# A four-layer graph network on one core: smaller reloads, a ring of four for the second step's projections, and one block of casts moved from layer 3 into layer 2's end

## The chip, the cores and the metric

The kernel runs on one core of a Trainium2 chip. The metric is the device time of the whole kernel in microseconds, the median of several runs. A profiled execution gives the span from the first to the last instruction and the trace that the views below are read from. The engines are named as in the profile: PE is TensorE (PEld its weight loads), DVE is VectorE, ACT is ScalarE, POOL is GpSimd, SP is SyncE, which here only issues DMAs.

## The reference

`x` has 4096 rows of 256 features, `adj` is a 4096 × 4096 matrix of zeros and ones. Four layers follow one another, each as `x = layernorm(x + layer(x))`:

```python
# layer 0: attention of 8 heads over the neighbours, softmax of leaky_relu(parent + child)
# layer 1: (diagonal + adj) @ (x @ weight) + bias
# layer 2: two steps
R = S + I;  R = R / R.sum(-1)              # S is adj
for n in range(2):
    A = top_p_attention(Xa, W1, W2, W3)    # softmax of q k^T, kept up to a mass of 0.9, renormalised
    Xf = R @ Xf
    Xa = A @ Xa
    Z = Z + Xf @ U1[n].T + Xa @ U2[n].T
x_out = layernorm_affine(X + Z)
# layer 3
agg = adj @ x / max(deg, 1)
out = relu(concat([x, agg]) @ W + b)
```

## The kernel before

The 4096 rows are 32 blocks of 128 (`NB` = 32). The change lies in layer 2 and at the start of layer 3.

**What is kept where.** `XD` holds, for each block of 128 source rows, two sets of 256 values as the moving operand of the matmuls. `X` holds the current attention features. `es[0..2]` are three tiles of 4096 numbers per partition, one row block of attention scores each, used in turn by row block modulo three. `kT` holds the keys of the step, transposed. `adj_piece` is a ring of three tiles of 256 KB; each takes four 128 × 128 blocks of the adjacency (f32) from DRAM. `work` is the pool of small tiles: `xb` (two buffers), `part` and `dif` (one each), `q` (two).

**One step of layer 2.** The step starts with projections: `project(step, b)` (L1441 to L1481) multiplies two row blocks with the step's weights. In step 1 it also reads back the running sum of these two blocks from DRAM into `xb` (SP, L1476), copies one half of the result into `X` (ACT) and the other into `part` or `dif` (ACT, L1479), adds it to `xb` on POOL (L1480) and writes the sum back with a DMA that POOL issues (L1481). There are sixteen such pairs. Then `keys` fills `kT`, and the main loop goes over row blocks `b`, each in eight slots `s`. In a row, PE computes the scores of row `b+2` (`scores`, L979, with ACT's exponentials L981 into `es[(b+2)%3]`), DVE finds the nucleus of row `b+1`, and PE transposes (`turn`, L1336) and multiplies (`gather`, L1345, eight matmuls) the kept attention of row `b`. Beside it, `diffusion` multiplies adjacency pieces with `XD` for row block `b+2` (step 0) or `b+3` (step 1): `piece` (L1531) issues the DMA on SP, `times` (L1540) the four matmuls. A `pieces` tuple says how many of these stand before the gather of each slot; a piece is loaded two ahead, as the ring has three.

**The order of the work.** Inside `manual_schedule` the order on each engine is the order of the program text. SP's queue is served in order: pieces, reloads, loads of `q` and `xb`, all stand one behind the other there.

**A step's end.** The rows of the last `diffusion` are done before the last attention rows, and `XD` must then be refilled with the results of this step (the next step's or layer 3's operand). `reload(rows_of, from, to)` (L1193 to L1197) brings those blocks from DRAM (`xfd` in step 0, `xtd` in step 1) with one DMA on SP of 256 KB per block. `freed` is a table of the slots (row counted from the end of the diffusion, slot) at which a group of four blocks is fetched. With the new blocks, `early` multiplies the first rows of the next step (step 0: rows 0 to 2) or of layer 3 (step 1: rows 0 to 4) beside the last attention rows: the list `todo` gives their order. The last blocks come by a reload after the loop (`NB - 4` on): in step 0 after `mend`, in step 1 after the last row's pieces.

**Layer 2's end and layer 3.** After the last row's `mend`, step 1 has a stretch of its own (L1764 to L1822): byte loads of the adjacency for layer 3 (`load_bytes`, `nas`), eight gathers of the last row with turns, the closing of rows 29, 30 and 31 (`closing`, `ahead3`, `weighted` L1438), the casts of layer 3's block 5 into `kT` (`cast3` L1842 on ACT), the remaining pieces of `todo`, the product of block 5 in four parts (`product(i)`, L1791, eight matmuls each from `a[i]`), and the last source block's matmuls (L1822) once row 31 is closed. Layer 3 then goes over the row blocks from 6 on: `ready(b)` casts a block's bytes into four `adj_piece` tiles (DVE L1840 and ACT L1842 in turn), `products(b)` makes 32 matmuls (L1873), `close(b)` makes the output rows. Blocks 6 and 7 are made ready ahead of the loop.

Of the kernel before, what the change touches and what calls it, by code (L numbers as in the profile page):

```python
# [9 lines left out]
F32 = mybir.dt.float32  # L10
I32 = mybir.dt.int32
F32R = mybir.dt.float32r
# [43 lines left out]
class Net:  # L56
# [745 lines left out]
    def layer2(self):  # L802
# [3 lines left out]
        with ExitStack() as ctx:  # L806
# [386 lines left out]
            def reload(src, a, b):  # L1193

                for k in range(a, b, 4):
                    to = min(k + 4, b)
                    nc.sync.dma_start(XD[:, k:to].bitcast(F32), src[k:to].rearrange("b p s d -> p b s d"))  # L1197
# [244 lines left out]
            def bank():  # L1442
                return psum.tile([P, 512], F32, name="ps_tp")

            def project(step, b):


                two = slice(b, b + 2)
                rows = lambda t: t.rearrange("b p d -> p b d")
                pl = psum.tile([P, 2, 512], F32, name="ps_logit", bufs=2)  # L1450
                if step == 0 and b < 16:
                    pt = bank()
                    for q in range(2):
                        for c in range(2):
                            nc.tensor.transpose(pt[:, (2 * q + c) * P:(2 * q + c + 1) * P],
                                                X[:, b + q, c * P:(c + 1) * P], self.ident)
                    xT = work.tile([P, 512], F32, name="aT", bufs=2)
                    nc.scalar.copy(xT, pt)
                    xT = xT.rearrange("p (q c m) -> p q c m", q=2, c=2)
                else:  # L1460
                    xT = held(step, b, 2)
                for q in range(2):
                    for c in range(2):
                        nc.tensor.matmul(pl[:, q, :], xT[:, q, c, :], wt[:, c].rearrange("p k m -> p (k m)"),
                                         start=(c == 0), stop=(c == 1))
                xb = work.tile([P, 2, D], F32, name="xb", bufs=2)
                if step == 0:
                    nc.scalar.copy(XD[:, two, 0, :], pl[:, :, :D])
                    nc.scalar.copy(xb, pl[:, :, D:])
                    nc.vector.tensor_sub(XD[:, two, 1, :], pl[:, :, :D], XD[:, two, 0, :].bitcast(F32))  # L1470
                    nc.scalar.dma_start(rows(pd[two]), xb)
                    xs = work.tile([P, 2, D], F32, name="part", bufs=1)
                    nc.gpsimd.tensor_add(xs, X[:, two, :], affine.unsqueeze(1).to_broadcast([P, 2, D]))
                    nc.gpsimd.dma_start(rows(xd[two, :, 1, :]), xs)
                else:
                    nc.sync.dma_start(xb, rows(xd[two, :, 0, :]))  # L1476
                    nc.scalar.copy(X[:, two, :], pl[:, :, :D])
                    xs = work.tile([P, 2, D], F32, name=("part", "dif")[b // 2 % 2], bufs=1)
                    nc.scalar.copy(xs, pl[:, :, D:])  # L1479
                    nc.gpsimd.tensor_add(xb, xb, xs)  # L1480
                    nc.gpsimd.dma_start(rows(xd[two, :, 0, :]), xb)  # L1481
# [23 lines left out]
            def ahead3(b, h, pz, last=False, queue=nc.scalar):  # L1505

                part = XD[:, b] if last else work.tile([P, 2, D], F32, name="part", bufs=1).bitcast(F32R)
                nc.scalar.copy(part[:, 0], pz[:, D:])
                nc.scalar.copy(h[:, 0], pz[:, :D])
                nc.vector.tensor_sub(part[:, 1], pz[:, D:], part[:, 0].bitcast(F32))  # L1510
                yield
                if not last:
                    queue.dma_start(xtd[at(b)].rearrange("o p s d -> (o p) s d"), part.bitcast(F32))
                queue.dma_start(xo[at(b), :, 1].rearrange("o p d -> (o p) d"), h[:, 0])
# [49 lines left out]
            for step in range(2):  # L1564
# [40 lines left out]
                if step == 0:  # L1605
# [3 lines left out]
                dd = 2 + step  # L1609
                rows_of = (xfd, xtd)[step]  # L1610
                banks, made = {}, []
                freed = ((-1, 4), (-1, 5), (-1, 6), (-1, 7), (0, 0), (0, 2), (0, 4)) if step == 0 else \
                    ((0, 4), (-1, 5), (-1, 6), (-1, 7), (0, 0), (0, 2), (1, 1))
                freed = {at: g for g, at in enumerate(freed)}
                if step == 0:
                    todo = [(k, g) for g in range(7) for k in range(3)]
                else:
# [5 lines left out]
                with tc.manual_schedule(engines=five):  # L1623
                    for b in range(NB - 1):
# [14 lines left out]
                        for s in range(8):  # L1639
# [28 lines left out]
                            for _ in range(pieces[s]):  # L1668
                                next(beside)
                            if (b + dd - NB, s) in freed:  # L1670
                                g = freed[b + dd - NB, s]
                                reload(rows_of, 4 * g, 4 * g + 4)
                            gather(pa, aTs.pop(0), s)
                            if s == 3 and step == 1 and b - 2 in done:
                                put = ahead3(b - 2, done.pop(b - 2), pz, queue=nc.gpsimd)
# [87 lines left out]
                with tc.manual_schedule(engines=five):  # L1763
                    nas = [t[:, i * 2048:(i + 1) * 2048].bitcast(U8).rearrange("p (k i) -> p k i", k=8)  # L1764
                           for t in (es[2], es[0]) for i in range(2)]
                    self.load_bytes(nas, 0, 0)
                    xb = bases(b)
                    h = done.pop(b - 2)
                    xT = turned(h[:, 0], bank())
                    pa = ps1.tile([P, 512], F32, name="ps_a")  # L1770
                    aTs = [turn(es[b % 3], 0)]
                    for g in range(8):
                        if g < 7:
                            aTs.append(turn(es[b % 3], g + 1))
                        if g in (0, 6):
                            put = ahead3(b - 2 + g // 6, h, weighted(xT, bank()))
                        gather(pa, aTs.pop(0), g)
                        if g in (0, 3):
                            next(close)
                        if g in (1, 7):  # L1780
                            whole(put)
                        if g == 5:
                            h = whole(close)
                            xT = turned(h[:, 0], bank())
                    close = closing(b, pa, r, xb)
                    ps = ps1.tile([P, 512], F32, name="ps_a")
                    a = [kT[:, i * 1024:(i + 1) * 1024].rearrange("p (k i) -> p k i", k=8) for i in range(4)]

                    def product(i):
                        for jc in range(8 * i, 8 * i + 8 - (i == 3)):  # L1790
                            nc.tensor.matmul(ps, a[i][:, jc % 8, :], XD[:, jc].rearrange("p s d -> p (s d)"),  # L1791
                                             start=(jc == 0), stop=False)

                    next(close)
                    next(close)
                    self.cast3(nas, 5, a, nc.scalar)
                    for _ in range(4):
                        next(beside)
                    next(close)
                    whole(beside)  # L1800
                    reload(xtd, NB - 4, NB - 1)
                    lasts = []
                    for k in range(2):
                        two = work.tile([P, 2, P], F32R, name="q", bufs=2)
                        nc.sync.dma_start(two.bitcast(F32), self.adjs[2 * k:2 * k + 2, :, NB - 1, :].rearrange("b p i -> p b i"))
                        lasts += [two[:, 0], two[:, 1]]
                    rows = [X[:, 8 * i:8 * i + 8, :].rearrange("p b d -> p (b d)").bitcast(U8)
                            .rearrange("p (k i) -> p k i", k=8) for i in range(4)]
                    product(0)
                    for k in range(5):  # L1810
                        t = piece(1, k, 7)
                        times(banks[k], t, 7, ks=range(3))
                    lasts.append(t[:, 3])
                    h = whole(close)
                    product(1)
                    xT = turned(h[:, 0], bank())
                    product(2)
                    pz = weighted(xT, bank())
                    product(3)
                    whole(ahead3(b, h, pz, True))  # L1820
                    for t, to in zip(lasts + [a[3][:, 7]], [banks[k] for k in range(5)] + [ps]):
                        nc.tensor.matmul(to, t, XD[:, b].rearrange("p s d -> p (s d)"), start=False, stop=True)  # L1822
                    self.load_bytes(rows, 1, 0)
                self.ahead3 = nas, rows
                self.early3 = [banks[k] for k in range(5)] + [ps]

    def load_bytes(self, nas, it, g):
# [17 lines left out]
    def layer3(self):  # L1845
        nc, tc, NB, D = self.nc, self.tc, self.NB, self.D
        G = 8
        with self.ctx3 as ctx:
# [6 lines left out]
            out = self.rows(self.out)  # L1855
            psum, ps1 = self.psum2, self.ps2
            nas = self.ahead3
            pieces = {}

            def ready(b):  # L1860
                it = b * P // self.IT
# [26 lines left out]
                self.layernorm(work, y, h)  # L1888
                nc.scalar.dma_start(out[:, b, :], y[:, 0])

            ready(6)
            ready(7)
            rest = [2, 5, 0, 1, 3, 4]
            for b in range(6, NB):
# [61 lines left out]
```

## Time and profile before

| what | value |
| --- | --- |
| median of three runs | 4033.21 us (4031.47 to 4039.32) |
| profiled execution, its own time | 4036.06 us |
| its span | 4034.4 us |
| mean granted PE clock | 0.987 |
| PE busy | 3912.9 us, 97% |
| DVE busy | 2994.1 us, 74% |
| ACT busy | 2757.1 us, 68% |
| POOL busy | 1088.5 us, 27% |
| step 0's end | about 2590 to 2720 us of the span |
| projections and keys of step 1 | about 2720 to 2835 us |
| loop of step 1 | about 2835 to 3790 us, 30.46 us a row |
| layer 2's end, then layer 3 | from about 3790 us; layer 3 from 3828 us |

The page of the profile gives busy times for the whole span. The views by window give waits ("engine, what ran, line, then what it waited for and its line: us in total, times, longest us"), and the timeline gives the start, the length, the engine, the line, the operation, output and inputs, shapes, the number of instructions taken together and, in brackets, the idle time before them and what ended it. In two rows of step 1, from 2900.00 to 2960.92 us, PE is busy all the time, DVE for 58.58, ACT for 53.71 and POOL for 34.40 us.

### The profile page before, as it was taken

Reading aid. Unit: us, or ns where it says so; the run is one execution under the profiler, and the core shown is the slowest. Engines: PE = TensorE matmul, PEld = TensorE weight load, DVE = VectorE, ACT = ScalarE, POOL = GpSimd, SP = SyncE. Lnnn points to the kernel's source line nnn. Section 1 sums busy time; section 2 is a strip of 40 time slices with the busy share of each in tenths; the row PEclk is TensorE's granted clock in tenths of the full one; section 3 lists DMA queues with packets and bytes.
Section 4 is the critical chain, followed back from the end, with each engine's and each line's share of the span. In section 5 each row is a group of like instructions: output and inputs, shape, how many; then the busy total and the mean of one; then the engine's idle time right before and its main releaser. Section 6 shows DMA issues by size and latency. Waiting matters only on the chain. (4 is left out here: it accounts for less than half of the span.)

```text
span 4034.4 us, 68767 instructions
## 1 busy us (share of the span) xinstructions
PE 3912.9 (97%) x25081; PEld 3383.5 (84%) x25081; DVE 2994.1 (74%) x6643; ACT 2757.1 (68%) x5127; POOL 1088.5 (27%) x1333
## 2 busy tenths in 40 slices
PE   8999999999999999899999999989999999999899
PEld 7899999999999788578888888865888888888687
DVE  7642328999999444567878788737899999999364
ACT  5543339999999322468888888825988888888132
POOL 0111110111333122301111111114555555555211
PEclk9999999999999999999999999999999999999999
DMA  4665547334222597432333232453333333335541
GB/s 136 224 214 175 178 147 228 93 101 131 69 76 64 192 369 311 131 115 95 98 97 101 95 104 92 146 190 100 103 116 103 106 119 99 107 120 188 185 152 47
DMA packets 320570, 556.42 MB, mean 138 GB/s; under 512 B 71558, under 2 KB 146198, under 8 KB 316118
## 3 DMA queue, kind: packets, MB, share of 16 engines
q1 hardware_dynamic: 239920, 395.13, 30.2%
q0 software_dynamic: 28336, 86.42, 6.5%
q10 hardware_dynamic: 51958, 70.29, 5.1%
q8 instruction: 203, 3.33, 0.3%
q14 instruction: 153, 1.25, 0.1%
HBM read 385.78 MB, written 165.94 MB: 137 GB/s over the span
## 5 line engine op out<-in xcount | busy, mean ns | idle before, releaser
L1345 PE MATMUL ps_a<-X,aT 128*128 128x256 f32 x4096 | 973.4, 380 | 1.3 <-ACT h L1486 1.1
L1345 PEld LDWEIGHTS ps_a<-X,aT 128*128 128x128 f32 x4096 | 776.5, 190 | 128.2 <-issue 3.5
L320 PE MATMUL acc<-gm,gt 128*128 128x198 bf16 x8192 | 706.2, 249 | 22.0 <-DMA gm<-gmd 6.8
L320 PEld LDWEIGHTS <-gt 128*128 128x128 fp8e4 x8192 | 702.8, 98 | 25.4 <-issue 9.8
L267 ACT ACTIVATE sg<-lpb,nlc 128x1024 fp8e4<-128x1024 f32 x636 | 667.2, 1135 | 61.5 <-DVE gt L269 39.8
L180 PE MATMUL ps_r<-XD,adj_piece 128*128 128x512 f32 x1888 | 528.4, 414 | 0.3 <-DMA adj_piece<-adjs 0.3
L538 PE MATMUL pz<-src,ar 128*128 128x264 f32 x4096 | 510.2, 287 | 15.2 <-DVE ar L528 12.7
L538 PEld LDWEIGHTS pz<-src,ar 128*128 128x128 f32 x4096 | 507.1, 190 | 18.1 <-DVE ar L528 11.6
L1072 ACT ACTIVATE ja<-e,nc 128x2048 uint8<-128x2048 f32 x240 | 480.9, 2004 | 2.0
L1338 ACT COPY aT<-ps_tp 128x512 f32<-128x512 f32 x512 | 296.4, 579 | 222.5 <-PE ps_tp L1336 220.5
L180 PEld LDWEIGHTS ps_r<-XD,adj_piece 128*128 128x128 f32 x1888 | 332.9, 189 | 69.3 <-issue 12.9
L531 ACT ACTIVATE nb<-a 128x512 uint8<-128x512 f32 x256 | 156.4, 630 | 287.7 <-DMA a<-in_adjt_dram 274.7
L1137 DVE MAX8 cand<-v 128x8 f32<-128x256 f32 x1024 | 347.3, 412 | 4.4
L1187 DVE SCALAR_TENSOR_TENSOR e<-e,edge 128x512 f32<-128x512 f32 x512 | 347.3, 750 | 2.2
L1336 PE MATMUL ps_tp<-ident,e 128*128 128x128 f32 x2048 | 307.9, 273 | 0.0
L1133 DVE SCALAR_TENSOR_TENSOR v<-e,hi 128x2048 f32<-128x2048 f32 x128 | 300.7, 2350 | 2.4
L1336 PEld LDWEIGHTS ps_tp<-ident,e 128*128 128x128 f32 x2048 | 257.1, 142 | 51.4 <-issue 0.7
L261 DVE TENSOR_SCALAR sg<-lpb,nlc 128x1024 fp8e4<-128x1024 f32 x384 | 285.4, 779 | 5.9 <-DVEq L358 3.9
L979 PE MATMUL ps_logit<-kT,q 128*128 128x512 f32 x1024 | 276.8, 412 | 12.4 <-DVE kT L937 8.0
L981 ACT ACTIVATE e<-ps_logit 128x1024 f32<-128x1024 f32 x256 | 260.2, 1027 | 30.3 <-PE ps_logit L979 30.3
L528 DVE CAST ar<-a 128x1024 fp32r<-128x1024 f32 x128 | 88.6, 693 | 231.0 <-PE pz L538 229.9
L790 PE MATMUL ps_adj<-XD,adj_piece 128*128 128x512 f32 x1024 | 244.9, 399 | 0.0
(397 smaller groups left out, 5543.7 us busy)
## 6 DMA issues: line engine op xcount, KB each, us to landing
adj_piece<-adjs SPq DMA_DIRECT2D x552, 256.0 KB, 2.7
a<-in_adjt_dram SPq DMA_DIRECT2D x256, 256.0 KB, 3.0
adjs<-adj_piece SPq DMA_DIRECT2D x96, 512.0 KB, 4.8
na<-nad SPq DMA_DIRECT2D x64, 512.0 KB, 3.7
nad<-nb POOLq DMA_DIRECT2D x128, 128.0 KB, 3.3
lpb<-lpd POOLq DMA_DIRECT2D x32, 512.0 KB, 4.1
na<-nad ACTq DMA_DIRECT2D x16, 1024.0 KB, 6.9
gmd<-gb ACTq DMA_DIRECT2D x64, 198.0 KB, 3.3
```

The costliest lines, as they stand in the source:

```text
L180: nc.tensor.matmul(ps, a[:, k, :], rhs(jc).rearrange("p s d -> p (s d)"), start=(jc == 0), stop=(jc == self.NB - 1))
L261: nc.vector.tensor_scalar(sg[:, k, :], lpb, nlc[:, 4 * g + k, h:h + 1], 2.0 ** -5, op0=ALU.is_ge, op1=ALU.mult, saturate=False)
L267: nc.scalar.activation(sg[:, k, :], lpb, AF.Sign, scale=-1.0, bias=nlc[:, 4 * g + k, h:h + 1], saturate=False)
L320: nc.tensor.matmul(acc[:, q, :6 * C1], gt[:, k, q * P:(q + 1) * P], gm0[:, k, :] if head0 else gm[:, jc, hh, :], start=(jc == 0 and q % 2 ...
L538: nc.tensor.matmul(pz[q][:, t, :W], ar[:, q, k, :], src[:, jc, t, s], start=(jc == 0 and s == 0), stop=(jc == NB - 1 and s == 1))
L1072: nc.scalar.activation(ja, e[:, s * HALF:(s + 1) * HALF], f, bias=nc1, accum_out=fs[:, i + s:i + s + 1])
L1133: nc.vector.scalar_tensor_tensor(v, ec, hi, ec, op0=ALU.is_lt, op1=ALU.mult, accum_out=sb[:, s:s + 1])
L1137: nc.vector.max(cand[:, 8 * j:8 * j + 8], v[:, k * 256:(k + 1) * 256])
L1187: nc.vector.scalar_tensor_tensor(ec, ec, edge[:, j:j + 1], ec, op0=ALU.is_ge, op1=ALU.mult)
L1336: nc.tensor.transpose(pt[:, k * P:(k + 1) * P], e[:, jc * P:(jc + 1) * P], self.ident)
L1338: nc.scalar.copy(aT, pt)
L1345: nc.tensor.matmul(pa[:, :D], aT[:, k * P:(k + 1) * P], X[:, jc, :], start=(jc == 0), stop=(jc == NB - 1))
```

## The change

There are three parts, all in layer 2 and its passage to layer 3.

1. In `project`, step 1, the pairs 2 to 12 take `xb` and the copied half from slots of `es[2]`, four deep each, in place of the work tiles `xb` (two buffers) and `part`/`dif` (one each). Pairs 0, 1 and 13 to 15 keep those.
2. `freed` gives a range of blocks for each slot. In step 0 the first 28 blocks come in ten reloads of one to four blocks where there were seven of four; in step 1 in twelve reloads of two or three blocks where there were seven of four.
3. In layer 2's end three pieces of `early` are multiplied between gathers (slots 3, 5, 7); blocks 28, 29 and 30 of `XD` are reloaded one by one (after gathers 2 and 4, and ahead of the last pieces) where one reload of three stood; the two loads of `q` tiles stand at gather 3; and the four casts of layer 3's block 6 are made there by ACT, into the `kT` tiles that `product` has read. Layer 3 starts with these (`pieces = {6: self.sixth}`) and makes only block 7 ready ahead of its loop.

```diff
@@ project
-                xb = work.tile([P, 2, D], F32, name="xb", bufs=2)
+                nth = (b - 16) % NB // 2
+                ring = [es[2][:, i + nth % 4 * 512:i + nth % 4 * 512 + 512].rearrange("p (q d) -> p q d", d=D)
+                        for i in (0, 2048)] if step and 2 <= nth <= 12 else ()
+                xb = ring[0] if ring else work.tile([P, 2, D], F32, name="xb", bufs=2)
...
-                    xs = work.tile([P, 2, D], F32, name=("part", "dif")[b // 2 % 2], bufs=1)
+                    xs = ring[1] if ring else work.tile([P, 2, D], F32, name=("part", "dif")[b // 2 % 2], bufs=1)
@@ main loop
-                freed = ((-1, 4), (-1, 5), (-1, 6), (-1, 7), (0, 0), (0, 2), (0, 4)) if step == 0 else \
-                    ((0, 4), (-1, 5), (-1, 6), (-1, 7), (0, 0), (0, 2), (1, 1))
-                freed = {at: g for g, at in enumerate(freed)}
+                if step == 0:
+                    freed = {(-1, 4): (0, 4), (-1, 5): (4, 7), (-1, 6): (7, 10), (-1, 7): (10, 14), (0, 0): (14, 18),
+                             (0, 1): (18, 21), (0, 2): (21, 23), (0, 3): (23, 25), (0, 4): (25, 27), (0, 5): (27, 28)}
+                else:
+                    freed = {(-1, 5): (4, 7), (-1, 6): (7, 10), (-1, 7): (10, 13), (0, 0): (13, 16), (0, 1): (16, 18),
+                             (0, 2): (18, 20), (0, 3): (20, 22), (0, 4): (22, 24), (0, 5): (0, 2), (0, 6): (2, 4),
+                             (1, 1): (24, 26), (1, 2): (26, 28)}
...
-                                g = freed[b + dd - NB, s]
-                                reload(rows_of, 4 * g, 4 * g + 4)
+                                reload(rows_of, *freed[b + dd - NB, s])
@@ layer 2's end
+                        if g in (3, 5, 7):
+                            next(beside)
                         gather(pa, aTs.pop(0), g)
+                        if g in (2, 4):
+                            k = NB - 5 + g // 2
+                            reload(xtd, k, k + 1)
+                        if g == 3:
+                            lasts = []
+                            for k in range(2):
+                                two = work.tile([P, 2, P], F32R, name="q", bufs=2)
+                                nc.sync.dma_start(two.bitcast(F32),
+                                                  self.adjs[2 * k:2 * k + 2, :, NB - 1, :].rearrange("b p i -> p b i"))
+                                lasts += [two[:, 0], two[:, 1]]
...
-                    for _ in range(4):
+                    for _ in range(3):
                         next(beside)
                     next(close)
+                    reload(xtd, NB - 2, NB - 1)
                     whole(beside)
-                    reload(xtd, NB - 4, NB - 1)
-                    lasts = []
-                    for k in range(2):
-                        two = work.tile([P, 2, P], F32R, name="q", bufs=2)
-                        nc.sync.dma_start(two.bitcast(F32), self.adjs[2 * k:2 * k + 2, :, NB - 1, :].rearrange("b p i -> p b i"))
-                        lasts += [two[:, 0], two[:, 1]]
...
                     lasts.append(t[:, 3])
+                    self.cast3(nas[:1], 6, a[:1], nc.scalar)
                     h = whole(close)
                     product(1)
                     xT = turned(h[:, 0], bank())
+                    self.cast3(nas[1:2], 6, a[1:2], nc.scalar)
                     product(2)
                     pz = weighted(xT, bank())
                     product(3)
+                    self.cast3(nas[2:3], 6, a[2:3], nc.scalar)
                     whole(ahead3(b, h, pz, True))
...
+                    self.cast3(nas[3:], 6, a[3:], nc.scalar)
                     self.load_bytes(rows, 1, 0)
-                self.ahead3 = nas, rows
+                self.ahead3, self.sixth = (nas, rows), a
@@ layer 3
-            pieces = {}
+            pieces = {6: self.sixth}
...
-            ready(6)
             ready(7)
```

## The prediction

> **What bounds the kernel now.** I read the page first. TensorE (PE) is busy 97% of the span, so apart from making its instructions fewer, which this change does not, time can only come from the idle 3% and from matmuls that run long. Next I read PE's waits in the three stretches that the diff touches, each in a window of its own.
>
> ```profile
> PE 3912.9 (97%) x25081; PEld 3383.5 (84%) x25081; DVE 2994.1 (74%) x6643; ACT 2757.1 (68%) x5127; POOL 1088.5 (27%) x1333
> ```
>
> Step 0's end (2590 to 2720 us) and the projections of step 1 (2720 to 2860):
>
> ```profile
> PE ps_logit L1540 <- DMA adj_piece<-adjs: 8.8, 4, 3.7
> ...
> PE ps_logit L979 <- ACT dif L1479: 3.1, 1, 3.1
> ...
> PE ps_logit L1464 <- ACT dif L1479: 1.8, 3, 0.8
> ```
>
> Layer 2's end and layer 3's start (3640 to 3860):
>
> ```profile
> PE ps_logit L1540 <- DMA adj_piece<-adjs: 5.8, 7, 2.1
> PE ps_tp L1873 <- DVE adj_piece L1840: 4.1, 1, 4.1
> ```
>
> From 2835 to 3640 us, step 1's loop, PE waits for nothing. The timeline of PE shows what the waits cost beyond their own length:
>
> ```profile
> 2637.43 2.07 PE L1540 MATMUL ps_logit<-XD,adj_piece 128*128 128x512 f32 x4 [3.73 <-DMA adj_piece<-adjs]
> 2639.30 3.62 PE L1345 MATMUL ps_a<-X,aT 128*128 128x256 f32 x8
> ...
> 2646.08 1.89 PE L1345 MATMUL ps_a<-X,aT 128*128 128x256 f32 x8
> ...
> 2652.39 1.40 PE L1540 MATMUL ps_logit<-XD,adj_piece 128*128 128x512 f32 x4 [2.12 <-DMA adj_piece<-adjs]
> 2653.58 3.39 PE L1345 MATMUL ps_a<-X,aT 128*128 128x256 f32 x8
> ...
> 2812.85 1.45 PE L979 MATMUL ps_logit<-kT,q 128*128 128x512 f32 x4 [3.07 <-ACT dif L1479]
> 2814.09 3.35 PE L1345 MATMUL ps_a<-X,aT 128*128 128x256 f32 x8
> ...
> 3828.33 17.83 PE L1873 MATMUL ps_tp<-XD,adj_piece 128*128 128x512 f32 x64 [4.14 <-DVE adj_piece L1840]
> ```
>
> A gather of eight takes 1.89 us, but 3.39 to 3.62 just after a gap. SP's timeline tells who caused the first two gaps: a reload of four XD blocks (1 MB) goes out just ahead of the piece.
>
> ```profile
> 2629.13 0.43 SPq L1197 DMA_DIRECT2D XD<-xfd  x1
> 2629.70 15.96 SPq L1531 DMA_DIRECT2D adj_piece<-adjs  x6
> 2645.71 0.43 SPq L1197 DMA_DIRECT2D XD<-xfd  x1
> ```
>
> **What the Trainium skill says.** "DMA: Bandwidth & Descriptors", "Queues, rings and completion order": one engine's hardware DMAs share one row of rings, consumed in ring order. The trace agrees: in the record of landings the reload of 2629.13 landed at 2636.73 (7.6 us), the piece behind it at 2637.38, 0.65 us later, and PE started at 2637.43. "TensorE: Matmul & The Clock Gate", "What's actually happening": after an idle window of about 3.4 us, free-running, PE runs at half rate. The trace agrees in kind: the granted clock is 0.54 in 2637.0–2643.5 and 0.83 in 3828–3846, yet a gap of 2.64 us at 2668.59 left none. "GPSIMD Engine Reference", "1. Specifications": POOL shares its SBUF interfaces with DVE instructions of two SBUF inputs. Agrees: POOL's add L1480 takes 1.26 us alone and 2.0 to 4.4 beside DVE's long operations.
>
> **Part 1, reloads of step 0 (`freed`).** Seven 1 MB reloads become ten of 0.25 to 1 MB over slots (−1,4) to (0,5); bytes are the same, three SP issues of about 0.4 us are added. The last 1 MB (blocks 28–31, after `mend`) stays. A piece is issued about 4.1 us before its need, since the ring has three. Behind a 1 MB reload it takes 7.6 or 6.0 plus 0.65: late by the gaps, 3.73 and 2.12. Those go: 5.85. The half rate with them: the step from 2637.43 to the next piece at 2643.19 is 5.76, where piece 1.02, gather 1.73 and turn 0.44 make 3.19, so 2.6; 2652.39 to 2657.16 is 4.77, so 1.6. Sum 10.1. In their place are reloads of 0.5 MB. No row shows one; above: the 1 MB in 6.0; below: a lone piece of 256 KB in 2.7. I take 4.5, with 0.65 behind it: 5.15 against 4.1, late by about 1 at one or two places; the quarter-size one at (0,5) lands in time. So −9 (−5 to −10). The third gap, 2.64, is behind the unchanged 1 MB and stays.
>
> **Part 2, ring of four in `project`.** Order on PE, ACT and POOL is unchanged, only the tiles are others. Before, ACT's copy L1479 waits for POOL's add two pairs earlier (dif 14.7 and part 8.9 us between 2750 and 2815), and POOL's add for SP's reload of xb (10 us, 8 times), whose slot frees only after POOL's write. PE waits behind ACT: 0.21, 0.79, 0.61, 0.36 at L1464 and 3.07 at the next score, and the gather at 2814.09 takes 3.35 for 1.89; with 0.3 on the score before it, 1.75. Sum 6.8. With rings of four, POOL lags instead: thirteen adds at 2 us and writes of 0.72 plus 0.3 are 39 us, against 52.7 us of 120 matmuls at 0.439, so it finishes near 2803. The ring's home es[2] is rewritten by the exponentials of score row 2 (near 2808): 4 to 5 us of margin. SP prefetches xb up to four ahead, but in its one queue q and the first pieces stand behind those loads; it has 50 us for them. Pairs 0, 1 and 13 to 15 keep the old buffers, whose tiles are long free when 13 comes. So −6.5 (−3 to −7).
>
> **Part 3a, reloads of step 1.** PE waits for no DMA there before; nothing to win. The end of the loop now has twelve reloads; the last, 0.5 MB, goes out about 4.9 us ahead of need: 0 to +1.5, I take +0.3. The five more 0.4 us issues are hidden by SP's slack.
>
> **Part 3b, layer 2's end.** From 3640 on, the end's stretch (the `weighted` matmuls of row 30 to the last q product) takes 35.5 us. Its PE work, from rows of the trace (gathers 1.73, turns 0.44, product groups 1.86 each, pieces of three matmuls 0.8, of four 1.0), sums to about 27. The gaps are five to seven waits for `adj_piece` (5.8) plus half rate (clock 0.93 in 3800–3826: 26 × 0.07 = 1.8). Three pieces go between gathers, where the ring's wait is covered by 2.2 us of gather and turn. The reload of three blocks (0.75 MB), which the wait of 2.10 at 3808.17 stood behind, is cut into singles at g=2, 4 and later, and the q tiles go ahead. The ring of three remains, and I leave 2.3 of waits. 35.5 − 27 − 2.3 = 6.2: −6 (−4 to −7).
>
> **Part 3c, block 6's casts.** Layer 3's first product waits 4.14 us for DVE's cast L1840 (0.70), after byte loads into `nas` that wait for layer 2's last work:
>
> ```profile
> 3821.91 4.85 DMA xo<-h
> ...
> 3827.53 0.70 DVE adj_piece L1840
> ...
> 3828.33 17.83 PE ps_tp L1873 x64
> ```
>
> 64 matmuls cost 2 × 7.47 = 14.93, as later blocks do; 17.83 is 2.9 more. The new casts are four ACT copies of 1.05 into kT pieces once `product(i)` has read them; ACT is under half busy there. The fourth, after the last matmul, is needed only by matmul 25 of block 6, 5.6 us later. `ready(7)` then starts about 3 us after the end and has 7.5. Gain 4.14 + 2.9 = 7.0; less up to 1.5 if PSUM's bank for block 8 waits for `close(2)`, whose x load stands behind the byte loads: −6.8 (−4 to −7).
>
> **Sum.** −9 − 6.5 + 0.3 − 6 − 6.8 = −28.0 on the profiled execution's 4036.06 (span 4034.4): 4008. The median of the runs shown is 2.85 lower (4033.21), giving 4005. As estimates of removed waits leave out the small ones put in their place, I add 2: **4007**.
>
> **Rivals.** *The small stalls keep the half rate* (chance 0.2): 0.5 MB reloads and a ring of three still make several 1 us waits, which are together within one clock window; half of parts 1 and 3b is lost: 7.5, and 4 of part 2 or 3c: about 4018. For it: a 2.12 gap was enough at 2652. Against: 2.64 was not at 2668. *DVE takes over the projections' end* (0.1): DVE row 2 starts when ACT's c is ready (wait 6.79 at 2839), and if DVE, which has 0.16 us a row to spare (58.58 busy of 60.92 in two rows, the rest being hand-overs), cannot start earlier, the 6.5 is given back: 4013. *Slower* (0.06): step 1's loop changes phase. A DVE operation of L995 takes 4.47 alone and 5.30 beside POOL's adds, so a shifted POOL can lengthen DVE's row of 30.3. From 31.46 on, 1.0 over PE's 30.46 in each of 28 rows, the 28 gained are used up; at 31.75 it is 36 lost, 8 slower: 4041. For it: the thin reserve. Against: POOL and DVE in that loop both follow PE, whose order there is unchanged, so the phases fall back into place. *The change does nothing* (0.04): the waits go over to the next transfer in SP's queue, since bytes are the same: 4030.
>
> **How the numbers follow.** Forecast 0.60, rivals 0.2, 0.1, 0.06, 0.04. The likeliest one's own range is from its parts: all at their best ends, −31.5, is 4002; at worse ends near −19, 4014. The branch waits on register jumps (3.9 and 1.9 us here) can move some us either way. Range for 8 in 10: 3999 to 4020. Within 0.2% (8.1 us, about what a measurement of this kernel can tell from no change) lies 4025 to 4041. Faster 0.89: forecast, half gain and DVE case less a little; same 0.05; slower 0.06.
>
> **What would show it.** Part 1: no wait over 1.5 us at L1540 before 2660, gathers at 1.9. Part 2: no PE wait for `dif` L1479; POOL's last ring write ends before the row‑2 exponentials. Part 3b: 29 us from `weighted` of row 30 to the end. Part 3c: L1873's first 64 matmuls in 15 us with a wait under 0.5. Wrong: step 1's loop at over 30.46 us a row, a new wait of PE for `e` L981 in row 2, or clock under 0.9 in these windows.

## The result and the profile after

The changed kernel takes 4016.49 us (median of five runs, 4013.26 to 4019.03) where the kernel before takes 4033.21 (4031.47 to 4039.32): a ratio of 0.9953, 95% interval 0.9939 to 0.9968, or 16.7 us less. Its profiled execution took 4013.26 us, span 4011.6, which is 22.8 us below the span before. That is more than the medians' 16.7 because this execution was the fastest of its five, 3.2 below their median, and the profiled one of the kernel before lies 2.85 above its median. A second comparison, on another occasion with both kernels side by side, gave 4012.61 us against 4036.06, ratio 0.9944 (0.9930 to 0.9958).

To see where the time went, the span is cut at starts of PE instructions that both timelines have: the first gather (`ps_a<-X,aT`, L1345) of a row, the first projection matmul (L1464), layer 3's first product. Each kernel has two profiles, the second taken with the experiments (on two different chips).

| stretch, us | before | changed |
| --- | --- | --- |
| start to layer 2's first projection (layers 0 and 1, not touched) | 1652.3 and 1652.9 | 1657.0 and 1653.9 |
| to row 30 of step 0 | 969.0 and 969.4 | 969.2 and 969.3 |
| row 30 to row 31 of step 0 | 53.0 and 54.0 | 44.7 and 46.1 |
| row 31 of step 0 to its last gather | 36.7 and 36.0 | 36.0 and 36.0 |
| on to step 1's first projection | 12.7 and 12.7 | 12.7 and 12.7 |
| first projection of step 1 to row 1 | 120.4 and 120.4 | 112.6 and 112.8 |
| row 1 to row 28 | 820.5 and 820.5 | 820.5 and 820.5 |
| row 28 to row 30 | 59.9 and 60.8 | 59.3 and 59.3 |
| row 30 to row 31 | 49.0 and 47.9 | 48.9 and 49.6 |
| row 31 to layer 3's first product | 55.0 and 56.1 | 47.8 and 47.5 |
| first 64 matmuls of layer 3 | 17.7 and 16.6 | 14.7 and 14.7 |
| rest | 188.4 and 188.4 | 188.4 and 188.4 |

The first pair of profiles lies 22.8 us apart, but layers 0 and 1, whose code is the same, were 4.6 us longer in the changed kernel's execution. From layer 2's first projection on, the changed kernel is 27.4 us shorter. In the second pair the spans lie 24.8 apart, layers 0 and 1 were 0.9 longer, and the rest is 25.7 shorter.

PE's waits in the changed kernel, in the window of step 0's end:

```profile
PE ps_logit L1543 <- DMA adj_piece<-adjs: 3.3, 3, 1.9
```

In the window of step 1's projections, all that is left over half a microsecond:

```profile
PE ps_logit L979 <- DVE kT L937: 4.4, 2, 3.8
```

From 3765 us to 3830, layer 2's end and layer 3's start:

```profile
PE ps_logit L1543 <- DMA adj_piece<-adjs: 3.5, 4, 1.5
```

The 8.8 at the early pieces became 3.3, the waits for `dif` are gone, the 4.1 for DVE's cast is gone, and 5.8 at the end became 3.5. PE's timeline after, at the places shown of before:

```profile
2639.13 1.20 PE L1543 MATMUL ps_logit<-XD,adj_piece 128*128 128x512 f32 x4 [0.69 <-DMA adj_piece<-adjs]
2640.17 1.89 PE L1345 MATMUL ps_a<-X,aT 128*128 128x256 f32 x8
...
2650.36 1.19 PE L1543 MATMUL ps_logit<-XD,adj_piece 128*128 128x512 f32 x4 [0.72 <-DMA adj_piece<-adjs]
2651.38 1.89 PE L1345 MATMUL ps_a<-X,aT 128*128 128x256 f32 x8
...
2664.13 3.42 PE L1543 MATMUL ps_logit<-XD,adj_piece 128*128 128x512 f32 x8 [1.88 <-DMA adj_piece<-adjs]
...
2748.85 52.15 PE L1464 MATMUL ps_logit<-wt,X 128*128 128x512 f32 x120 [0.21 <-ACT e L981]
...
2803.57 1.89 PE L1345 MATMUL ps_a<-X,aT 128*128 128x256 f32 x8
...
3808.48 7.41 PE L1890 MATMUL ps_tp<-XD,kT 128*128 128x512 f32 x32
3815.74 7.63 PE L1890 MATMUL ps_tp<-XD,adj_piece 128*128 128x512 f32 x32
```

The gathers behind the small gaps run at 1.89, all 120 projection matmuls run through in one piece, and layer 3 starts without a wait, from `kT`. The third gap, behind the last 1 MB reload of step 0, is still there (1.88; 2.55 in the second profile), and eight matmuls after it take 3.42 in place of 2.11. Granted clock in the windows that showed 0.54 and 0.68 before:

```profile
2637.00:2643.50 6.50, 5.81 (x29) 4.54 (x27) 5.93 (x28) 0.85 (x2) 1.34 (x4) 1.00 0.83 292
2652.00:2657.30 5.30, 5.30 (x28) 4.43 (x28) 0.00 (x0) 0.59 (x1) 0.00 (x0) 1.00 0.73 229
```

(Columns: window and length, busy time and count of PE, PEld, DVE, ACT and POOL, clock, DMA share, GB/s.)

### The profile page after: what moved, and what is told of

Same layout as the page of the kernel before. It is cut to its first block, busy times and chain, and to the rows that moved or that the text cites. A ratio compares the mean times of both kernels' runs of the same rounds, so it can differ in the third digit from the quotient of the medians.

```text
span 4011.6 us, 68787 instructions
## 1 busy us (share of the span) xinstructions
PE 3907.3 (97%) x25081; PEld 3382.3 (84%) x25081; DVE 2996.9 (75%) x6641; ACT 2757.9 (69%) x5129; POOL 1115.9 (28%) x1333
## 5 line engine op out<-in xcount | busy, mean ns | idle before, releaser
L1345 PE MATMUL ps_a<-X,aT 128*128 128x256 f32 x4096 | 968.9, 379 | 1.3 <-ACT h L1489 1.1
L1345 PEld LDWEIGHTS ps_a<-X,aT 128*128 128x128 f32 x4096 | 773.2, 190 | 127.2 <-issue 3.6
L180 PE MATMUL ps_r<-XD,adj_piece 128*128 128x512 f32 x1888 | 528.4, 414 | 0.0
L180 PEld LDWEIGHTS ps_r<-XD,adj_piece 128*128 128x128 f32 x1888 | 332.9, 189 | 68.8 <-issue 12.9
```

The costliest lines, as they stand in the source:

```text
L180: nc.tensor.matmul(ps, a[:, k, :], rhs(jc).rearrange("p s d -> p (s d)"), start=(jc == 0), stop=(jc == self.NB - 1))
L1345: nc.tensor.matmul(pa[:, :D], aT[:, k * P:(k + 1) * P], X[:, jc, :], start=(jc == 0), stop=(jc == NB - 1))
```

## The experiments

The theory was that the parts add, each worth what its stretch shows, and that the difference between spans and medians comes from stretches with unchanged code. The rival was that an undone part costs less than its stretch, since another wait takes its place. Each experiment starts from the changed kernel unless said otherwise. Ratios are to the kernel before, run beside the experiment. The unaltered changed kernel was run beside three of the experiments only (1 MB reloads for the second time, and the two with the mixed end), so for the others the stretch is the measure and the total decides little.

**The ring undone.**

```diff
-                        for i in (0, 2048)] if step and 2 <= nth <= 12 else ()
+                        for i in (0, 2048)] if step and 2 <= nth <= 1 else ()
```

> The changed kernel with the old buffers in every pair of step 1's projections (part 2 undone alone). Theory, parts add: the stretch from the first projection of step 1 to the gathers of row 1 takes 120.4 us as in the kernel before, where the changed kernel takes 112.6; PE waits again for dif L1479 (about 5 us with the row's first score) and one half-rate window of 3.41 us comes back; total about 7.7 us over the changed kernel's 4016.5, so 4024. Rival, DVE sets the start of step 1's loop: less than 3 us, 4018 to 4019.

Measured: the stretch 118.9 us, +6.2 to +6.3; median 4020.07, ratio to the kernel before 0.9956 (0.9939 to 0.9972). The waits for `dif` and `part` come back, without the half-rate window on row 0, which in the kernel before was another 1.5. The rival (under 3) falls for the stretch; the ratio overlaps with the changed kernel's, so the total does not show it.

**One half of the ring at a time.** First only `xb` in the ring, then only the copied half.

```diff
-                    xs = ring[1] if ring else work.tile([P, 2, D], F32, name=("part", "dif")[b // 2 % 2], bufs=1)
+                    xs = work.tile([P, 2, D], F32, name=("part", "dif")[b // 2 % 2], bufs=1)
```

> The changed kernel with only xb in the ring of four; the copied half is again in part and dif, one buffer each. Theory: the round trip of an xb slot (add, write back, next load) paces POOL in the kernel before, so four xb slots alone bring most: from the first projection of step 1 to row 1 at most 114.5 us (112.6 changed, 118.9 with no ring, 120.4 before). Rival: the copies into part and dif, each waiting for the add two pairs earlier, are the bound whatever xb does: 117 or more.

```diff
-                xb = ring[0] if ring else work.tile([P, 2, D], F32, name="xb", bufs=2)
+                xb = work.tile([P, 2, D], F32, name="xb", bufs=2)
```

> The changed kernel with only the copied half in the ring of four; xb again in two work tiles. Theory: POOL still waits for the loads of xb, ACT is only let run two pairs further ahead of it: the same stretch at 115 to 118.5 us, and POOL's backlog ends later, so the exponentials of score row 2 may wait for it. Rival: depth of the copied half was the bound: 112.6 to 113.5.

Measured: 113.6 us with `xb` alone (median 4008.76, ratio 0.9939, 0.9921 to 0.9957), 121.7 with the copied half alone (4018.26, 0.9962, 0.9948 to 0.9976). So `xb`'s depth is nearly the whole matter (6.8 of the 7.7 us; PE still waits once for `part`, 0.3), and the copied half by itself brings nothing. The runs of these two kernels, on one chip, do not overlap (4002.1 to 4012.9 and 4016.0 to 4021.2): here the total shows it too. PE's waits in the projections' window with the copied half alone in the ring:

```profile
PE ps_logit L979 <- ACT dif L1482: 5.9, 1, 5.9
```

and POOL's, in the same kernel and then in the one with `xb` alone:

```profile
POOL xb L1483 <- DMA xb<-xd: 12.5, 9, 2.9
```

```profile
POOL xb L1483 <- DMA xb<-xd: 1.4, 1, 1.4
```

With two `xb` slots POOL waits nine times for a reload. Letting ACT run ahead only gathers the small stalls (1.76 us in three, and 3.07, before) into one of 5.9 behind the ring's end: pair 13 finds `dif` free, but pair 15 takes it again, and ACT's copy waits for POOL's add of pair 13:

```profile
2802.05 0.59 ACT L1482 COPY dif<-ps_logit 128x512 f32<-128x512 f32 x1 [6.40 <-POOL xb L1483]
```

The expectation's upper bound for the copied half, 118.5, was exceeded: it is no better than no ring at all.

**Step 0's reloads as before.**

```diff
-                    freed = {(-1, 4): (0, 4), (-1, 5): (4, 7), (-1, 6): (7, 10), (-1, 7): (10, 14), (0, 0): (14, 18),
-                             (0, 1): (18, 21), (0, 2): (21, 23), (0, 3): (23, 25), (0, 4): (25, 27), (0, 5): (27, 28)}
+                    freed = ((-1, 4), (-1, 5), (-1, 6), (-1, 7), (0, 0), (0, 2), (0, 4))
+                    freed = {at: (4 * g, 4 * g + 4) for g, at in enumerate(freed)}
```

> The changed kernel with step 0's reloads again as seven of 1 MB in the old slots (the first part of the freed table undone alone). Theory: from row 30's first gather to row 31's in step 0 it takes 53.0 us as before in place of 44.7, with two waits of 2 to 4 us for adj_piece at the early pieces and two spells at half rate; total +9, 4025. Rival, the half-rate spells were luck of the window: only the waits come back, +5 to 6, 4022.

Measured: the stretch 51.3 us, +6.7 on the first profile of the changed kernel, but the median was 4015.54 (ratio 0.9942, 0.9926 to 0.9959), no slower than the changed kernel's 4016.49 measured at another time. Profile and median spoke against each other, so the kernel was run again beside an unaltered copy of the changed one.

> The changed kernel once more, unaltered, for the same chip as the runs beside it. Theory, the parts add and the unchanged layers 0 and 1 vary by chance (their length was 1652.0 to 1658.3 us in six profiles): 18 to 26 us under the kernel before on this chip, and from row 30 to row 31 in step 0 44 to 47 us. Rival, the program is really 4.6 us slower in layers 0 and 1 than the kernel before: their length is again near 1657.

> Step 0's reloads as seven of 1 MB again, the same kernel as e2_reloads_1mb, beside the changed kernel on one chip. Its first profile had +6.7 us from row 30 to row 31 in step 0 and yet its times were those of the changed kernel. Theory, part 1 is worth what the stretch shows: 5 to 8 us slower than after_again in the median, and the stretch again at 50 to 53. Rival, the waits behind 1 MB reloads vary from execution to execution and the profile caught a bad one: the stretch under 49, the median within 3 us of after_again.

Measured: 4012.61 for the changed kernel and 4016.19 for this one, 3.6 apart (six runs each, 4009.5 to 4017.0 and 4014.6 to 4023.4; ratios to the kernel before 0.9944, 0.9930 to 0.9958, and 0.9954, 0.9940 to 0.9969). The stretch was 50.5 here and 46.1 there. PE's timeline of the second run with 1 MB reloads:

```profile
2639.20 1.21 PE L1543 MATMUL ps_logit<-XD,adj_piece 128*128 128x512 f32 x4 [2.51 <-DMA adj_piece<-adjs]
2640.25 1.89 PE L1345 MATMUL ps_a<-X,aT 128*128 128x256 f32 x8
...
2651.60 1.60 PE L1543 MATMUL ps_logit<-XD,adj_piece 128*128 128x512 f32 x4 [2.20 <-DMA adj_piece<-adjs]
2653.00 3.17 PE L1345 MATMUL ps_a<-X,aT 128*128 128x256 f32 x8
```

The waits behind 1 MB reloads came back in both profiles. Over all profiles the stretch is 50.5 to 54.0 us in the four with 1 MB reloads (mean 52.2) and 43.7 to 46.7 in the nine that have the changed table (mean 45.2; the last-reload variant below is left out): 7.0 us, without overlap. So the rival's "under 49" did not occur, while the medians, 3.6 apart, show less than the theory's 5 to 8. How much of the 7.0 the executions without a profile kept is not seen.

**Layer 2's end in the old order, casts of block 6 kept.** The three `next(beside)`, the single reloads and the `q` loads go back.

```diff
-                        if g in (3, 5, 7):
-                            next(beside)
...
-                        if g in (2, 4):
-                            k = NB - 5 + g // 2
-                            reload(xtd, k, k + 1)
...
-                    reload(xtd, NB - 2, NB - 1)
                     whole(beside)
+                    reload(xtd, NB - 4, NB - 1)
```

> The changed kernel with the pieces, reloads and q loads of layer 2's end in the old order, but block 6's casts still there. Theory, read from the two traces: of the 7.2 us saved up to layer 3's first matmul, 4.1 are the cast's wait, so this part alone is worth 3.1: from row 31's first gather of step 1 to layer 3's first product about 50.9 us against 47.8 changed and 55.0 before; total 4019 to 4020. Rival, the forecast's size: the order is worth 6 to 7, 4023.

Measured: 50.5 us from row 31 to layer 3, +2.7 to +3.0: the smaller size, not the forecast's. Median 4016.27 (ratio 0.9946, 0.9929 to 0.9963). PE's waits from 3775 us:

```profile
PE ps_logit L1543 <- DMA adj_piece<-adjs: 6.1, 7, 2.6
```

The longest, 2.6 behind the reload of three blocks, is 1.5 at that place in the changed kernel, and the six others, 3.5 together, are three with 2.1 there. The pieces between gathers, the single reloads and the `q` loads went back together, so what each is worth is not shown.

**Block 6's casts in layer 3 again.**

```diff
-                    self.cast3(nas[:1], 6, a[:1], nc.scalar)
...
-            pieces = {6: self.sixth}
+            pieces = {}
...
+            ready(6)
             ready(7)
```

> The changed kernel with block 6's casts again in layer 3 (its first ready). Theory: the first product waits about 4 us for DVE's cast, and then runs its first 64 matmuls at 17.8 us in place of 14.7, as before: +7.1, 4023 to 4024. Rival: with the end's transfers earlier, the bytes and DVE are ready sooner, so the wait is under 2 us and no half-rate spell follows: +1 to 2, 4018.

Measured: +3.0 to +3.3 to layer 3's first product and +1.65 in its first 64 matmuls, together about 4.8; median 4019.08 (ratio 0.9953, 0.9936 to 0.9969). PE's timeline:

```profile
3808.51 0.40 PE L1835 MATMUL ps_a<-XD,kT 128*128 128x512 f32 x1
3812.47 16.56 PE L1886 MATMUL ps_tp<-XD,adj_piece 128*128 128x512 f32 x64 [3.56 <-DVE adj_piece L1853]
```

The wait comes back nearly whole (3.56 for 4.14); the half-rate spell was one window of 3.41 us, where the first profile before had two (6.83) and the second before one.

**Step 1's reloads as before.**

```diff
-                    freed = {(-1, 5): (4, 7), (-1, 6): (7, 10), (-1, 7): (10, 13), (0, 0): (13, 16), (0, 1): (16, 18),
-                             (0, 2): (18, 20), (0, 3): (20, 22), (0, 4): (22, 24), (0, 5): (0, 2), (0, 6): (2, 4),
-                             (1, 1): (24, 26), (1, 2): (26, 28)}
+                    freed = ((0, 4), (-1, 5), (-1, 6), (-1, 7), (0, 0), (0, 2), (1, 1))
+                    freed = {at: (4 * g, 4 * g + 4) for g, at in enumerate(freed)}
```

> The changed kernel with step 1's reloads again as seven of 1 MB in the old slots. Theory: no wait of PE stood there, so only the 0.5 us that rows 28 to 30 of step 1 took more before (59.85 against 59.32) come back; total within 1 us of the changed kernel. Rival: the small reloads are also what lets the last row's pieces arrive in time, so rows 30 to 31 or the end lengthen by 2 us or more.

Measured: rows 28 to 30 in 59.3 us as in the changed kernel, rows 30 to 31 in 48.5, the end (whose code is the changed kernel's) in 45.7; median 4014.63 (ratio 0.9948, 0.9930 to 0.9965). The small reloads of step 1 bring nothing that this profile shows. The end is 1.8 to 2.1 shorter than in the changed kernel's two profiles. Its waits are 3.0 in place of 3.5 and 3.7, and no half-rate window fell into it; the same holds for the profile with `xb` alone in the ring (45.8, waits of 3.1). The 0.5 and 1.5 us that the two profiles of before have more in rows 28 to 30 stand at a late piece of the diffusion (L180, waits of 0.3 and 1.3), which did not recur here with the same reload sizes; why is open.

**The kernel before, once more.**

> The kernel before once more, for a second profile. Theory: layers 0 and 1 vary by chance (1652.3 in its first profile, 1652 to 1658 in nine others of the same code), from row 30 to row 31 in step 0 it is 50 to 53 us, from the first projection to row 1 120.4, from row 31 of step 1 to layer 3 55. Rival: the kernel before is really shorter in layers 0 and 1, 1652 again.

Measured: one run, 4037.31 us; its stretches are in the table. Layers 0 and 1 took 1652.9, near the rival's 1652. The range over fourteen profiles is 1649.6 to 1658.3, the mean 1654.5. Both profiles of before lie under it, but so do four of the other twelve (1649.6, 1649.7, 1652.0, 1653.9), which run the same code there. The time that PE spent at half rate in that part goes with it.

**A mixed end.** Two matmuls of block 5's product stand before each of the last eight pieces.

```diff
-                    whole(beside)
...
-                    product(0)
+                    for k in range(3):
+                        product(0, slice(2 * k, 2 * k + 2))
+                        next(beside, None)
+                    whole(beside)
                     for k in range(5):
+                        product((k + 3) // 4, slice((2 * k + 6) % 8, (2 * k + 6) % 8 + 2))
                         t = piece(1, k, 7)
...
-                    product(1)
                     xT = turned(h[:, 0], bank())
```

> The changed kernel with the first two parts of block 5's product spread, two matmuls at a time, between the last eight adjacency pieces of layer 2's end. Theory: the ring of three is late there because pieces stand 0.7 to 1.0 us apart; at 1.2 to 1.4 apart the four waits (0.96, 0.77, 1.46, 0.36) shrink to 1 in all, and the half-rate window of 3.41 us behind them goes: -2.5 to -4.3 us in the stretch from row 31's first gather to layer 3's first product (47.8 in the changed kernel). Rival: the transfers are limited by bandwidth there, with the byte loads of layer 3 beside them, and the waits stay: 0 to -1.

Measured: 43.9 us from row 31 to layer 3, 3.7 to 3.9 less than in the two profiles of the changed kernel. Its waits there:

```profile
PE ps_logit L1543 <- DMA adj_piece<-adjs: 1.3, 3, 0.5
```

The rival, bandwidth, falls: the bytes are the same, only the deadlines moved, and the waits went from 3.5 to 1.3. The half-rate window (at 3797.8 in the changed kernel's first profile) did not appear, here or in the next experiment; but two of the eight profiles with the changed kernel's end lack it as well, and those ends took 45.7 and 45.8. Against them the mixed end is 1.8 to 2.0 shorter, about what the waits lost (3.0 and 3.1 there, 1.3 here); that it also prevents the window is not shown. Median 4010.07 (ratio 0.9937, 0.9922 to 0.9953) against 4012.61 on the same chip; the runs overlap (4004.8 to 4018.0 and 4009.5 to 4017.0), so the total is not settled.

**The mixed end and the last reload of step 0 in three parts.**

```diff
-                             (0, 1): (18, 21), (0, 2): (21, 23), (0, 3): (23, 25), (0, 4): (25, 27), (0, 5): (27, 28)}
+                             (0, 1): (18, 21), (0, 2): (21, 23), (0, 3): (23, 25), (0, 4): (25, 27), (0, 5): (27, 28),
+                             (0, 6): (28, 30), (0, 7): (30, 31)}
...
-                    reload(rows_of, NB - 4, NB)
+                    reload(rows_of, NB - 1, NB)
```

> The mixed end of e8_mixed_end, and the last reload of step 0 (blocks 28 to 31, 1 MB ahead of the row's last pieces) in three parts: 28 and 29 at slot 6 of the last row, 30 at slot 7, 31 where the whole stood. Theory: the wait of 1.88 us behind the 1 MB reload at the step's end goes, and with it the half rate after it (1.4 us): -2 to -3 us from row 30 to the gathers' end of row 31, where the changed kernel takes 80.6; with the end's -2.5 to -4.3, 5 to 7 us under the changed kernel. Rival: the moved transfers make the pieces of slots 6 and 7 late in its place, 0 in that stretch.

Measured: row 30 to row 31's last gather in 81.4 us, where the changed kernel takes 80.6 and 82.2 and the mixed end alone 81.3: nothing. Median 4010.43 (ratio 0.9938, 0.9924 to 0.9952). PE's timeline:

```profile
2665.35 0.50 PE L1543 MATMUL ps_r<-XD,adj_piece 128*128 128x512 f32 x1 [0.65 <-DMA adj_piece<-adjs]
2667.18 0.96 PE L1543 MATMUL ps_r<-XD,adj_piece 128*128 128x512 f32 x3 [1.33 <-PEq L1203]
```

The wait of 1.88 for the piece has gone over to PE's branch at `mend` (0.30 before, 1.33 now) and 0.65 of a piece, 1.98 for 2.18. That the flag which the branch reads was nearly as late as the transfer is read from these waits, not tested. The rival named the result and not the cause.

## Why the prediction was right, and where its sizes were off

The direction, the range (3999 to 4020) and the places hold. The sum was −28.0 from layer 2 on; the profiles show −27.4 and −25.7 there. That it came so near is partly luck: part 3b fell short by 2.9 in the first pair, and part 2's surplus (1.2), part 3c's (0.3) and 1.2 us in places where nothing was forecast (row 31 of step 0, rows 28 to 30 of step 1) made up for most of it. The first median, 4016.5, lies outside the forecast's own 4002 to 4014 (its best ends add to −31.0, not −31.5, which leaves the 4002); the range that held was widened for the rivals. By its steps:

- **Part 1, −9.** 8.3 and 7.9 in the two pairs; 7.0 over thirteen profiles. The gaps of about 1 us that were allowed for small reloads are there (0.69 and 0.72, in the second profile 1.30 and 0.78). The mis-sized term is the half rate: 4.2 us was to go with the two gaps, but in the changed kernel's two profiles a window stands behind the third gap, which brought none in the first profile before. By an estimate from the trace (half of PE's busy time in half-rate windows), half rate cost 4.5 us from row 30 to row 31 before and 1.6 after. Nor is 7.6 us what 1 MB takes by itself: the trace counts sixteen completions for each transfer, of the reload issued at 2629.13 fifteen by 2634.59 and the last at 2636.73, of the piece behind it fifteen by 2635.23 and the last at 2637.38. So 2.1 of the 3.73 us were one late part of sixteen; the other three profiles with 1 MB reloads have 3.51, 2.79 and 2.51 there.
- **Part 2, −6.5.** 7.7. The reasoning, that POOL's wait for reloads of `xb` is at the root and ACT and PE only queue behind it, is shown by the two half rings. The sum had row 0's half-rate window in it (1.75 for the slow gather and the score; row 0 to row 1 went from 30.0 to 28.5), and 0.21 too much: that wait is for the exponentials and is still there. The surplus lies ahead of row 0, where 6.2 us went for 4.8 of waits; by the same estimate half rate is 0.9 of the rest, and what remains is open. POOL's last write from the ring was issued at 2797.2, and PE did not wait for the exponentials beyond the 0.3 and 0.2 that were there before.
- **Part 3a, +0.3.** Nothing shown.
- **Part 3b, −6.** This is the term that failed in size: 3.1 in the first pair (7.2 to layer 3's start less the 4.14 of the cast), 4.8 in the second (8.6 less 3.8), where the end before had twice the time at half rate, and, undone, 2.7 to 3.0. "I leave 2.3 of waits" was too little: 3.5 to 3.7 were left, since three pieces in a ring of three arrive no faster where they stand 0.7 to 1.0 us apart. And the half rate that was to go, 1.8, stayed as one window, about 1.7. The mixed end, which spreads just those pieces, takes 2.2 off the waits. The sign named for this part, 29 us from row 30's `weighted` to the end, did not come: it is 30.7, with two pieces moved ahead of that stretch.
- **Part 3c, −6.8.** 4.14 and 2.95, or 7.1, in the first pair, 3.8 and 1.8 in the second; undone, 4.8. Layer 3 did not wait for block 7 or 8.
- **The rivals.** The half rate behind short stalls did occur, behind the third gap of step 0 and at layer 2's end, where it took some 1.7 of the 2.9 us that part 3b lacks; behind part 1's two gaps it did not. Its 4018 is nearer to the first median than the forecast is, but the stretches lost less than it says. DVE did not take over: rows 1 to 28 take 820.47 us in every profile, which also disposes of the slower loop. That the waits go over to the next transfer and nothing is won is excluded by the ratios.
- **The base.** The forecast for the median was 9.5 us lower than the first measurement and 5.6 lower than the second. Little of it is in the sum's places (0.6 and 2.3 by the profiles). The step that failed is the last, "The median of the runs shown is 2.85 lower": it takes the distance of one profiled execution from a median as fixed, while layers 0 and 1 alone move by 8.7 us between executions of the same code, and the base profile was 2.1 below their mean. The kernel before itself had medians of 4033.2 to 4036.1 in four groups of runs, the changed one 4016.5 and 4012.6. What the executions without a profile did by stretch can't be seen, so how the medians' 16.7 and 23.5 and the profiles' 27.4 and 25.7 meet is argued, not shown.

## What to carry to other kernels

Cost a change by stretches between fixed instructions, and compare stretches: here a part worth 3 us is plain in its stretch and invisible in a median that code elsewhere moves by 8. Take more than one profile and count half-rate windows apart from waits: layer 2's end, with the same code, took 45.7 to 48.8 us in eight profiles, and its waits only 3.0 to 3.8. When a ring is too short, find which buffer's round trip includes a store and a reload; deepening the buffer behind it here only moved the stall to the end of the ring. And where a ring of transfers can't grow, spread the consumers: two matmuls in between took the waits from 3.5 to 1.3 us.

## What was not expected of the hardware

The same gap does not always bring the half rate: gaps of 2.79 and 2.51 us at the first early piece were followed by gathers of 1.89, one of 3.73 by 3.62, and one of 2.12 at the next by 3.39. The record of granted clocks tells why. Its half-rate spells are one to three windows of 3.41 us, and within a trace they all start on one grid of that step. What counts is how long PE idles inside one window of the grid. In the kernel before, the gap of 2.12 us lies in one window; that of 2.64 is cut in two by a boundary (0.91 and 1.73):

```profile
2649.79:2653.20 3.41, 1.28 (x7) 1.00 0.93 344
2653.20:2656.61 3.41, 3.41 (x10) 0.50 0.23 77
...
2663.45:2666.86 3.41, 2.50 (x11) 1.00 0.85 310
2666.86:2670.27 3.41, 1.68 (x7) 1.00 0.43 142
2670.27:2673.68 3.41, 2.83 (x14) 1.00 0.43 139
```

(Columns: window and length, busy time and count of PE, clock, DMA share, GB/s.) From layer 2's first projection on, in all fourteen traces, each of the 59 full-rate windows in which PE idled 1.85 us or more was followed by one at half rate, none of the 9377 with under 1 us was, and of the 82 between them 23 were. So the whole idle window of 3.4 us that the prediction starts from is not needed. Where the grid lies differs from execution to execution (its offset from the first instruction is 0.0 to 3.4 us in the fourteen traces), so which of the stalls is hit is chance.

- Code that is the same in fourteen profiles took 1649.6 to 1658.3 us, the longer the more of it ran at half rate (44 to 68 us by the record of granted clocks; correlation 0.83).
- One loop of 27 rows took 820.47 us in all fourteen, to the hundredth: PE waited for nothing there and ran at full rate throughout.
